# Two 16-head attention stages of a one-core transformer chain: the order of TensorE's products within a turn

## The chip, the cores and the metric

The kernel runs on one core of one Trainium2 chip. The metric is the device time in microseconds (us) of one execution. The other cores of the chip are not used. TensorE (PE in the profile, PEld for its weight loads), VectorE (DVE), ScalarE (ACT), GpSimd (POOL) and the DMA queue of SyncE (SP) each work through their own instructions in order and wait for one another by semaphores.

## The reference

The reference is a chain of eight blocks over x of 16 sequences x 256 positions x 128 features: four attention-like blocks and four feed-forward blocks, each with a layer norm ahead of it and behind it and a residual sum. Two of the eight have a 16-head causal attention with 8 features a head. The first of them (block five) is, cut to what matters:

```python
q = (x @ Wq).reshape(b, t, 16, 8) * 8 ** -0.25
k = (x @ Wk).reshape(b, t, 16, 8) * 8 ** -0.25
v = (x @ Wv).reshape(b, t, 16, 8)
dot = jnp.einsum('bqhd,bkhd->bhqk', q, k)
dot = jnp.where(causal, dot, -jnp.inf)
attn = jax.nn.softmax(dot, axis=-1)
out = jnp.einsum('bhqk,bkhd->bqhd', attn, v).reshape(b, t, 128) @ Wo
```

The second (inside block seven, behind a scan) has the same products with rotated and normalized queries and keys and with four key heads shared by the sixteen query heads. The change touches these two attentions alone.

## The kernel before

**Tiles.** The 16 sequences are handled as NG = 8 groups g of two sequences (512 positions). Within a group each sequence b = 0, 1 is one batch of attention. The 16 heads lie as 4 rows r of 32 partitions by 4 variants v of 8 features: `km` and `qm` (`variants`, line 377) are copies of the keys and queries, masked so that one variant's 8 features are left.

**One batch** (`attention`, line 434) has these steps; I give each group of TensorE products a name for the rest of the text.
- Scores by query (lines 449 to 461), three times (i = 0, 1, 2): four products, one a row, of 32 partitions, `qT` by `km`, each into a PSUM bank of its own (named Q in the prediction), then for each row a causal mask, added by a product of the identity with `negmask` (M), then VectorE's `tensor_reduce` for the maxima (`at_nm`).
- GpSimd splits the maxima into three bf16 pieces (`at_pc`, lines 464 to 469); TensorE transposes them and ScalarE makes four scaled copies (`at_mT`, lines 471 to 476).
- Scores by key (lines 481 to 502), three times: four products `kT` by `qm` (K), four that subtract the maxima, `ones` by `at_mT` (R), ScalarE's exponential into `at_e`, GpSimd's `affine_select` for the causal part.
- Values' products (lines 505 to 518; V): `at_vm` by `at_e`, each with 32 output partitions, into one PSUM bank "o", in six steps.
- ScalarE copies the bank to `at_oT` (line 521), TensorE transposes it (525), VectorE makes reciprocals and quotients (`at_rec`, `at_y`, lines 530 to 532), TensorE transposes `at_y` (537), ScalarE copies it to `at_yT`.

**PSUM.** Both stages use RING_BANKS (line 37): one bank "o" and a ring of seven banks "s" from which all other products take theirs in order. A product into a bank waits until the reader of the bank's last content is done.

**The order.** Each batch, each group's head and each tail is a Python generator; a `yield` ends a step. The head (`head`, line 1287 in the first stage and 1636 in the second) makes `kT`, `qT`, `km`, `qm` and `at_vm` of a group ahead of its batches; the tail (lines 1320 and 1662) multiplies with `Wo` and normalizes. `turns` (line 392) runs them: in each turn every item whose start has come runs its next step, in the order of the list, the latest batch first, then older batches, then heads, then one generator `beside`. Batch b of group g starts in turn 12g + 6b, so twelve turns are one group. Scores by query fall on even turns, scores by key on odd ones, values on both. The order in which the steps are run is the order of the instructions on every engine, since `manual_schedule` leaves it as it is. So an even turn of the steady part reads, on TensorE: Q, M, then values, then others; an odd turn: K, R, values, others. "Others" (X) are the transposes and projections of heads, tails and of the batches' last steps. Their places within the twelve turns are, in the first stage: `at_pc` and `at_y` in turns 2 and 8, `wk` 8, `wq` 9, `wo` 10, `at_oT` 5 and 11, `wv` and the transposes of `xn` 6. VectorE makes `at_y` in turns 1 and 7 and `xn` in turn 5.

The masks of one turn, before, follow their row's product:

```python
for k, s in zip(rows, ss, strict=True):
    self.mm(s, qT[k, q], km[k, vs, keys], True, False)
for r, s in enumerate(ss):
    ...
    self.mm(s[:, :, t * P :], ident, bc(negmask, 1, n), False, True)
    v_.tensor_reduce(nm[:, t, r, vs], s, AX.X, ALU.max, negate=True)
```

Of the kernel before, what the change touches and what calls it, by code (L numbers as in the profile page):

```python
# [29 lines left out]
NB, SEQ, P, D = 16, 256, 128, 128  # L30
NG, NT, GT = 8, 4, 512
# [154 lines left out]
def idle(n):  # L186

    for _ in range(n):
        yield


def bc(ap, axis, n):

    ap = ap.unsqueeze(axis)
    shape = list(ap.shape)
    shape[axis] = n
    return ap.to_broadcast(shape)


class Ctx:  # L200
# [188 lines left out]
        lo = 16 * (v % 2)  # L389
        self.nc.scalar.copy(to[:, :, :, lo : lo + 8], src)  # L390

    def turns(self, items):


        now = 0
        items = [[start, 0, steps] for start, steps in items]
        while items:
            for item in items[:]:
                for _ in range(min(3, now - item[0] + 1 - item[1])):
                    item[1] += 1  # L400
                    if next(item[2], self) is self:
                        items.remove(item)
                        break
            now += 1

    def attention_stage(self, head, early, first, tail, beside=iter(())):

        got = [{} for _ in range(NG)]
        heads = [head(g, got[g]) for g in range(NG)]
        for _ in range(first):
            next(heads[0])
        self.attention_pools()  # L420
        for _ in heads[0]:
            pass

        def batch(g, b):
            yield from self.attention(g, b, got[g])
            if b == 1:
                yield from tail(g, got[g]["yT"])

        items = [(12 * g + 6 * b, batch(g, b)) for g in range(NG) for b in range(2)]
        items = items[::-1] + [(12 * g - early, heads[g]) for g in range(1, NG)] + [(9, beside)]  # L430
        with self.tc.manual_schedule():
            self.turns(items)

    def attention(self, g, b, got):

        nc, v_ = self.nc, self.nc.vector
        vm = self.vm[g % 2]
        qT, kT, km = (got[n] for n in ("qT", "kT", "km"))
        ident, negmask, ones = self.cb["ident"], self.cb["negmask"], self.cb["rows"]
        q0, q1 = (slice((2 * b + t) * P, (2 * b + t + 1) * P) for t in range(2))
        both = slice(2 * b * P, (2 * b + 2) * P)
        rows = [slice(32 * r, 32 * r + 32) for r in range(4)]
        nm = self.t([P, 2, 4, 4], "at_nm", 2)
        for i in range(3):

            t, q, keys, vs = (0, q0, q0, slice(0, 4)) if i == 0 else (1, q1, both, slice(2 * i - 2, 2 * i))
            ss = [self.ps("s") for _ in rows]
            for k, s in zip(rows, ss, strict=True):
                self.mm(s, qT[k, q], km[k, vs, keys], True, False)
            for r, s in enumerate(ss):
                n = vs.stop - vs.start
                s = s.rearrange("p (v n) -> p v n", v=n)
                self.mm(s[:, :, t * P :], ident, bc(negmask, 1, n), False, True)
                v_.tensor_reduce(nm[:, t, r, vs], s, AX.X, ALU.max, negate=True)  # L459
            if i < 2:  # L460
                yield from idle(2)
        yield

        pc = self.pieces[b]
        for i in range(3):
            at = pc[:, :, :, 4 * i : 4 * i + 4]
            nc.gpsimd.tensor_copy(at, nm)
            if i < 2:
                nc.gpsimd.tensor_tensor(nm, nm, at, ALU.subtract)
        yield from idle(3)  # L470
        tp = self.ps("mm")
        for t in range(2):
            self.mm(tp[:, t * P : (t + 1) * P], pc[:, t].rearrange("p r n -> p (r n)"), ident, True, True)
        mT = self.t([P, 4, SEQ], "at_mT", 2, dt=BF16)
        for v in range(4):
            nc.scalar.activation(mT[:, v, :], tp[:, :SEQ], AF.Copy, scale=self.sel[:, v : v + 1])
        yield from idle(3)


        es, qm = [], got["qm"]  # L480
        for i in range(3):
            vs, to = (slice(2 * i, 2 * i + 2), slice(0, SEQ)) if i < 2 else (slice(0, 4), slice(P, SEQ))
            keys, queries = (q0, both) if i < 2 else (q1, q1)
            ss = [self.ps("s") for _ in range(4)]
            for k, s in zip(rows, ss, strict=True):
                self.mm(s, kT[k, keys], qm[k, vs, queries], True, False)
            for k, s in zip(rows, ss, strict=True):
                self.mm(s, ones[k, :], mT[k, vs, to], False, True)
            e = self.t([P, 4, GT], "at_e", 4)
            for r, s in enumerate(ss):  # L490
                nc.scalar.activation(e[:, r], s, AF.Exp)  # L491

            if i < 2:
                at, n = e.rearrange("p r (v t n) -> p r v t n", v=2, t=2)[:, :, :, 0, :], 2
            else:
                at, n = e.rearrange("p r (v n) -> p r v n", v=4), 4
            nc.gpsimd.affine_select(  # L497
                at, at, [[0, 4], [0, n], [1, P]], ALU.is_ge, 0.0, base=0, channel_multiplier=-1
            )
            es.append(e)  # L500
            if i < 2:
                yield from idle(2)
        yield

        o = self.ps("o")
        for v in range(4):
            reg = SEQ * (v // 2)
            for r, k in enumerate(rows):
                e = es[v // 2][:, r].rearrange("p (v n) -> p v n", v=2)[:, v % 2, :]
                self.mm(o[k, reg : reg + SEQ], vm[:, 2 * b, v, k], e, v == 0, False)  # L510
            yield
        for v in range(4):
            reg = SEQ * (v // 2)
            for r, k in enumerate(rows):
                e = es[2][:, r].rearrange("p (v n) -> p v n", v=4)[:, v, :]
                self.mm(o[k, reg + P : reg + SEQ], vm[:, 2 * b + 1, v, k], e, False, v % 2 == 1)
            if v % 2:
                yield

        oT = self.t([P, GT], "at_oT", 1)  # L520
        nc.scalar.copy(oT, o)  # L521
        yield
        tp = self.ps("mm")
        for j in range(4):
            nc.tensor.transpose(tp[:, j * P : (j + 1) * P], oT[:, j * P : (j + 1) * P], self.c["ident"])
        yield from idle(2)
        y = self.t([P, 2, 4, 2, 2, 8], "at_y", 2)
        tp = tp.rearrange("p (w t r u n) -> p w t r u n", w=2, t=2, r=4, u=2)
        rec = self.t([P, 2, 2, 4, 2], "at_rec", 2)
        v_.reciprocal(rec, tp[:, :, :, :, :, 8])  # L530
        for w in range(2):
            v_.tensor_tensor(y[:, :, :, w], tp[:, w, :, :, :, 0:8], bc(rec[:, w], 4, 8), ALU.mult)
        yield
        tp = self.ps("mm")
        for t in range(2):
            at = y[:, t].rearrange("p r w u n -> p (r w u n)")
            nc.tensor.transpose(tp[:, t * P : (t + 1) * P], at, self.c["ident"])
        if b == 0:
            got["yT"] = self.t([P, GT], "at_yT", 2)
        nc.scalar.copy(got["yT"][:, both], tp[:, :SEQ])  # L540
        yield
# [1545 lines left out]
```

## Time and profile before

| what | us |
|---|---|
| median of 3 runs | 2942.89 (2938.27 to 2943.25) |
| the profiled execution | 2940.6 |
| its span, first to last instruction | 2938.8 |
| busy: PE, DVE, ACT, POOL | 2729.7, 1953.3, 1717.5, 1017.2 |
| first attention stage, from its first masks to its last values | 1525.8 to about 1835 |
| second attention stage | 2326.2 to about 2640 |

Names in the profile are the program's tiles: `ps_s` is a bank of the ring, `ps_o` the values' bank. Nearly all products are issued by the helper at line 336, so they are told apart by their tiles. A shape such as 32*128 is rows by columns of the array that the product uses. A product of two float32 operands shows as two matmul instructions, so a group of four appears as x8. The end of a matmul is modelled; the distance from the start of one row to the start of the next is measured.

### The profile page before, as it was taken

The page shows a single profiled execution, that of the slowest core. Times are in us where ns is not written, and L with a number is a line of the kernel's source. Part 1 is how long each engine was busy: PE and PEld are TensorE (multiplying, and loading weights), DVE is VectorE, ACT ScalarE, POOL GpSimd, SP SyncE. Part 2 cuts the span into 40 slices and gives each one's busy share as a digit, 9 for nine tenths or more (in the row PEclk, how much of TensorE's full clock was granted, in tenths as well). Part 3 has the DMA queues.
Part 4 walks back from the last instruction along what each step waited for, and adds up shares of the span by engine and source line. Part 5 has one row for each costly group of instructions (what it writes and reads, how often), then busy time and mean ns, then how long its engine had stood idle before and what let it go on. Part 6 is the DMA issues. An engine that isn't in the chain of part 4 may idle for free.

```text
span 2938.8 us, 59589 instructions
## 1 busy us (share of the span) xinstructions
PE 2729.7 (93%) x23673; PEld 1845.0 (63%) x23674; DVE 1953.3 (66%) x5309; ACT 1717.5 (58%) x3568; POOL 1017.2 (35%) x1406
## 2 busy tenths in 40 slices
PE   8889999999998799999978998899999799989998
PEld 4556667766666588888853443566666444436897
DVE  5665666666675989999866765666574677736542
ACT  6756566666665567777735665444444277756443
POOL 3543333333345100000044555422231466545332
PEclk9999999999999899999988999899999899999999
DMA  4000000000000000000020000000000000010000
GB/s 117 12 1 1 2 1 2 2 2 2 5 12 24 1 16 9 8 9 8 9 71 5 1 1 1 1 1 1 1 1 1 2 1 1 1 33 27 2 16 16
DMA packets 29150, 31.30 MB, mean 11 GB/s; under 512 B 7292, under 2 KB 20156, under 8 KB 28732
## 3 DMA queue, kind: packets, MB, share of 16 engines
q1 hardware_dynamic: 28872, 27.49, 3.1%
q8 instruction: 187, 3.06, 0.4%
q14 instruction: 91, 0.75, 0.1%
HBM read 23.29 MB, written 4.19 MB: 9 GB/s over the span
## 4 chain that ended last, share of the span: by engine, by line
PE 69%; ACT 12%; DVE 11%; POOL 5%; issue 2%; DMA 0%; POOLq 0%; SPq 0%; ACTq 0%; DVEq 0%
PE ps_s L336 44%; PE ps_o L336 10%; PE ps_mm L336 6%; PE ps_s L325 3%; ACT e L949 2%; ACT at_e L491 1%; POOL ln_rs L245 1%; ACT lg L1215 1%; DVE xn L264 1%; PE ps_xin L336 1%; ACT meT L1222 1%; POOL e L952 1%; PE ps_sum L336 1%; ACT L949 1%; ACT mdisp L1122 1%
## 5 line engine op out<-in xcount | busy, mean ns | idle before, releaser
L459 DVE TENSOR_REDUCE at_nm<-ps_s 128x2 f32<-128x512 f32 (+1 forms) x384 | 238.1, 682 | 119.6 <-PE ps_s L336 119.6
L491 ACT ACTIVATE at_e<-ps_s 128x512 f32<-128x512 f32 x384 | 198.2, 604 | 97.0 <-PE ps_s L336 94.8
L1504 DVE TENSOR_TENSOR scan<-ps_s,lm 128x384 f32<-128x384 f32 x256 | 124.7, 549 | 142.4 <-PE ps_s L336 142.1
L497 POOL TENSOR_SCALAR_AFFINE_SELECT at_e<-at_e 128x1024 f32<-128x1024 f32 (+1 forms) x96 | 135.1, 1407 | 209.0 <-ACT at_e L491 208.7
L245 POOL TENSOR_TENSOR ln_rs<-ln_rs,mhalf 128x4 f32<-128x4 f32 x192 | 196.1, 1021 | 15.8
L1031 POOL TENSOR_TENSOR ln_rs<-ln_mv,mendt 128x4 f32<-128x4 f32 x6 | 1.2, 200 | 521.0 <-DVE ln_mv L1029 521.0
L244 POOL TENSOR_SCALAR ln_rs<-ln_mv 128x4 f32<-128x4 f32 x184 | 39.6, 215 | 371.2 <-DVE ln_mv L257 352.8
L336 PE MATMUL ps_o<-my,meT 128*128 128x129 f32 x1024 | 142.5, 286 | 22.2 <-ACT mgot L1234 18.4
L336 PE MATMUL ps_s<-l1f_phi,mxT 128*128 128x256 f32 x512 | 141.6, 401 | 21.6 <-DVE mpart L1096 15.9
L899 DVE TENSOR_REDUCE l_max<-ps_s 128x3 f32<-128x384 f32 x256 | 124.8, 551 | 51.4 <-PE ps_s L336 49.1
L952 POOL TENSOR_SCALAR_AFFINE_SELECT e<-e 128x512 f32<-128x512 f32 x128 | 78.9, 637 | 217.2 <-ACT e L949 217.2
L336 PEld LDWEIGHTS ps_o<-my,meT 128*128 128x128 f32 x1024 | 126.3, 193 | 40.5 <-ACT mgot L1234 24.1
L336 PE MATMUL ps_s<-qm,kT 32*128 32x512 f32 x768 | 144.0, 652 | 8.0 <-DVE at_nm L459 7.8
L336 PE MATMUL ps_s<-km,qT 32*128 32x512 f32 x768 | 138.2, 667 | 11.3 <-DVE qT L1648 3.7
L336 PEld LDWEIGHTS ps_o<-l_w,mlp_h 128*128 128x128 f32 x1024 | 126.0, 192 | 19.1 <-issue 12.8
L336 PE MATMUL ps_o<-at_e,at_vm 128*32 128x128 f32 (+1 forms) x2048 | 123.2, 338 | 15.3 <-ACT at_oT L521 15.3
L336 PE MATMUL ps_o<-l_w,mlp_h 128*128 128x128 f32 x1024 | 130.1, 276 | 4.0 <-ACT oT L969 3.9
L336 PE MATMUL ps_s<-b_negmask,b_ident 128*128 128x256 bf16 (+1 forms) x640 | 123.6, 303 | 8.1 <-DVE b_negmask L780 1.4
L1481 ACT COPY BT<-ps_s 128x512 f32<-128x512 f32 x64 | 37.5, 587 | 158.1 <-PE ps_s L336 158.1
L336 PE MATMUL ps_mm<-mdisp,mxn 128*128 128x128 f32 x1024 | 125.3, 279 | 5.0 <-DVE mdisp L1134 4.9
L336 PEld LDWEIGHTS ps_mm<-mdisp,mxn 128*128 128x128 f32 x1024 | 121.8, 195 | 7.9 <-DVE mdisp L1134 6.6
L336 PE MATMUL ps_s<-xT,l_w 128*128 128x512 f32 x256 | 124.4, 607 | 1.3 <-ACT xT L811 1.3
(469 smaller groups left out, 7192.5 us busy)
## 6 DMA issues: line engine op xcount, KB each, us to landing
mw<-in_l1fw SPq DMA_DIRECT2D x16, 256.0 KB, 2.6
moe_w<-in_moe SPq DMA_DIRECT2D x16, 256.0 KB, 5.3
l_w<-in_l SPq DMA_DIRECT2D x10, 256.0 KB, 3.3
x<-in_x SPq DMA_DIRECT2D x8, 256.0 KB, 5.1
xs<-x SPq DMA_DIRECT2D x8, 256.0 KB, 2.1
out<-x SPq DMA_DIRECT2D x8, 256.0 KB, 2.3
slT<-xs SPq DMA_DIRECT2D x6, 256.0 KB, 2.8
l1f_phi<-in_l1f SPq DMA_DIRECT2D x1, 1024.0 KB, 5.0
```

What stands on the lines that cost most here:

```text
L244: g.tensor_scalar(out, in_, scale, eps, ALU.mult, ALU.add)
L245: g.tensor_tensor(out, out, self.mhalf[:, :n], ALU.pow)
L325: self.nc.tensor.transpose(out[:n, k * P : (k + 1) * P], src[:, k, cols], self.c["ident"])
L336: self.nc.tensor.matmul(out, lhsT=lhsT, rhs=rhs, start=start, stop=stop, skip_group_check=True)
L459: v_.tensor_reduce(nm[:, t, r, vs], s, AX.X, ALU.max, negate=True)
L491: nc.scalar.activation(e[:, r], s, AF.Exp)
L497: nc.gpsimd.affine_select(at, at, [[0, 4], [0, n], [1, P]], ALU.is_ge, 0.0, base=0, channel_multiplier=-1)
L899: v.tensor_reduce(mx[:, b, :, h, 16], s, AX.X, ALU.max, negate=True)
L949: nc.scalar.activation(e[:, h].rearrange("p j n -> p (j n)"), s[:, : 3 * P], AF.Exp)
L952: nc.gpsimd.affine_select(e[:, :, j, :], e[:, :, j, :], [[0, 4], [1, P]], ALU.is_ge, 0.0, base=0, channel_multiplier=-1)
L1481: nc.scalar.copy(s, ps)
L1504: v.tensor_tensor(m, s[:, : SEQ + P], lm[:, SCAN_HEADS[4 * (t // 2) + 2 * i + hh], :], ALU.mult)
```

## The change

`turns` can be given, for even and for odd turns, an order of kinds. Each step now yields the kind of the step that follows it ("by query", "values", "by key", or None for others), and in each turn the items are sorted by that order (items of one kind keep the list's order). In even turns it is others, by query, values, by key; in odd ones values, by key, others, by query. So on TensorE an even turn becomes X, M, Q, V, and an odd one V, K, R, X: over two turns X, M, Q, V, V, K, R, X. Every step stays in its turn. Within a step of scores by query the four masks are now issued first (they start the bank) and the four products after them; the four reductions follow the four products. On VectorE the order of instructions in the steady part of the first stage stays as it was; on GpSimd the `affine_select` of an odd turn now stands ahead of the pieces `at_pc` of that turn. In the two instruction orders that are built, the array's tile shape changes 283 and 291 times between neighbouring products of the two stages before, and 195 times in each after.

```diff
@@ -389,21 +389,28 @@
         lo = 16 * (v % 2)
         self.nc.scalar.copy(to[:, :, :, lo : lo + 8], src)
-    def turns(self, items):
+    def turns(self, items, kinds=None):
         now = 0
-        items = [[start, 0, steps] for start, steps in items]
+        items = [[item[0], 0, item[1], item[2] if len(item) > 2 else None] for item in items]
         while items:
-            for item in items[:]:
+            order = items[:]
+            if kinds:
+                order.sort(key=lambda item: kinds[now % 2].index(item[3]))
+            for item in order:
                 for _ in range(min(3, now - item[0] + 1 - item[1])):
                     item[1] += 1
-                    if next(item[2], self) is self:
+                    item[3] = next(item[2], self)
+                    if item[3] is self:
                         items.remove(item)
                         break
             now += 1
     def attention_stage(self, head, early, first, tail, beside=iter(())):
@@ -426,10 +433,10 @@
             if b == 1:
                 yield from tail(g, got[g]["yT"])
-        items = [(12 * g + 6 * b, batch(g, b)) for g in range(NG) for b in range(2)]
+        items = [(12 * g + 6 * b, batch(g, b), "by query") for g in range(NG) for b in range(2)]
         items = items[::-1] + [(12 * g - early, heads[g]) for g in range(1, NG)] + [(9, beside)]
         with self.tc.manual_schedule():
-            self.turns(items)
+            self.turns(items, ([None, "by query", "values", "by key"], ["values", "by key", None, "by query"]))
     def attention(self, g, b, got):
@@ -450,16 +457,18 @@
             t, q, keys, vs = (0, q0, q0, slice(0, 4)) if i == 0 else (1, q1, both, slice(2 * i - 2, 2 * i))
             ss = [self.ps("s") for _ in rows]
+            n = vs.stop - vs.start
+            by_variant = [s.rearrange("p (v n) -> p v n", v=n) for s in ss]
+            for s in by_variant:
+                self.mm(s[:, :, t * P :], ident, bc(negmask, 1, n), True, False)
             for k, s in zip(rows, ss, strict=True):
-                self.mm(s, qT[k, q], km[k, vs, keys], True, False)
-            for r, s in enumerate(ss):
-                n = vs.stop - vs.start
-                s = s.rearrange("p (v n) -> p v n", v=n)
-                self.mm(s[:, :, t * P :], ident, bc(negmask, 1, n), False, True)
+                self.mm(s, qT[k, q], km[k, vs, keys], False, True)
+            for r, s in enumerate(by_variant):
                 v_.tensor_reduce(nm[:, t, r, vs], s, AX.X, ALU.max, negate=True)
+            yield
             if i < 2:
-                yield from idle(2)
-        yield
+                yield "by query"
         pc = self.pieces[b]
         for i in range(3):
@@ -474,7 +483,8 @@
         mT = self.t([P, 4, SEQ], "at_mT", 2, dt=BF16)
         for v in range(4):
             nc.scalar.activation(mT[:, v, :], tp[:, :SEQ], AF.Copy, scale=self.sel[:, v : v + 1])
-        yield from idle(3)
+        yield from idle(2)
+        yield "by key"
         es, qm = [], got["qm"]
@@ -499,8 +509,9 @@
             )
             es.append(e)
             if i < 2:
-                yield from idle(2)
-        yield
+                yield
+                yield "by key"
+        yield "values"
         o = self.ps("o")
         for v in range(4):
@@ -508,14 +519,14 @@
             for r, k in enumerate(rows):
                 e = es[v // 2][:, r].rearrange("p (v n) -> p v n", v=2)[:, v % 2, :]
                 self.mm(o[k, reg : reg + SEQ], vm[:, 2 * b, v, k], e, v == 0, False)
-            yield
+            yield "values"
         for v in range(4):
             reg = SEQ * (v // 2)
             for r, k in enumerate(rows):
                 e = es[2][:, r].rearrange("p (v n) -> p v n", v=4)[:, v, :]
                 self.mm(o[k, reg + P : reg + SEQ], vm[:, 2 * b + 1, v, k], e, False, v % 2 == 1)
             if v % 2:
-                yield
+                yield "values" if v == 1 else None
         oT = self.t([P, GT], "at_oT", 1)
         nc.scalar.copy(oT, o)
```

## Prediction

> **What bounds the kernel now.** I read the page first, then the stretches of the two stages that the change touches, then the order of work on PE, DVE and POOL inside one period.
>
> ```profile
> span 2938.8 us, 59589 instructions
> L459 DVE TENSOR_REDUCE at_nm<-ps_s 128x2 f32<-128x512 f32 (+1 forms) x384 | 238.1, 682 | 119.6 <-PE ps_s L336 119.6
> L491 ACT ACTIVATE at_e<-ps_s 128x512 f32<-128x512 f32 x384 | 198.2, 604 | 97.0 <-PE ps_s L336 94.8
> ```
>
> The profiled execution took 2940.6 us (span 2938.8); the median of the three runs is 2942.9, so this profile stands 0.1% below it. Both groups mostly wait for PE. The stages' steady parts confirm it (columns: length, busy PE, PEld, DVE, ACT, POOL, clock):
>
> ```profile
> 1593.38:1797.04 203.66, 201.16 (x1816) 89.63 (x1813) 141.31 (x321) 130.49 (x285) 110.63 (x152) 1.00 0.01 1
> 2394.48:2590.00 195.52, 190.35 (x1711) 86.29 (x1707) 136.58 (x216) 140.01 (x318) 116.72 (x138) 0.99 0.01 1
> ```
>
> PE is busy 97 to 99%, but a busy PE is not a full one. Its timeline (start, length; I call masks M, scores by query Q, scores by key K, their at_mT products R, values' products V, all else X):
>
> ```profile
> 1655.37 0.40 PE L336 MATMUL ps_s<-at_mT,b_rows 32*128 32x512 bf16 x4
> 1655.70 0.65 PE L336 MATMUL ps_o<-at_e,at_vm 128*32 128x128 f32 x16
> 1656.27 1.12 PE L336 MATMUL ps_s<-xT,l_wq 128*128 128x512 f32 x2
> 1657.33 1.14 PE L336 MATMUL ps_s<-km,qT 32*128 32x512 f32 x8
> 1658.40 0.61 PE L336 MATMUL ps_s<-b_negmask,b_ident 128*128 128x256 bf16 x4
> 1658.94 0.64 PE L336 MATMUL ps_o<-at_e,at_vm 128*32 128x256 f32 x8
> 1659.51 1.16 PE L336 MATMUL ps_s<-l_wo,at_yT 128*128 128x128 f32 x8
> 1660.60 1.55 PE L336 MATMUL ps_s<-qm,kT 32*128 32x512 f32 x7
> 1661.56 0.63 PE L336 MATMUL ps_s<-at_mT,b_rows 32*128 32x512 bf16 x3
> 1661.99 0.59 PE L336 MATMUL ps_s<-qm,kT 32*128 32x512 f32 x1
> ```
>
> The tile shape (32*128, 128*128, 128*32) changes at almost every row. From start to start: M 0.54 before V but 0.45 before another 128*128 group (1651.95 to 1652.40), so 0.09 goes to the change of shape; wo to K is 1.09 where eight products of that shape (l_wv, before more 128*128 work) take 0.995. I price a change at 0.095. The last three rows show the second loss: the fourth K is late, because its PSUM bank still awaits a DVE reduction. Such a split costs about 0.77 (K and R together 2.1 instead of 1.29); it occurs 18 times in 37 between 1580 and 1800 and 8 in 37 between 2380 and 2600.
>
> **The change part by part.** No instruction is added or removed. *Changes of shape*: the built order of PE has 283 of them in the first stage and 291 in the second, and 195 in each afterwards: 184 x 0.095 = -17.5 us if PE alone counted. Here two rules of the Trainium skill disagree. "TensorE: Matmul & The Clock Gate" (Part 2, NX overlap) has the drain of one matmul hide under the next one's fill: then the sum is 0. "TensorEngine Tiling" (Key Properties) says a change of mode drains the array. The rows above side with the second, so I take -17.5. *Masks ahead of the products*: same eight instructions; a late bank now delays a mask, which are serial anyway. But the four products now end together and the first reduction starts later. "TensorEngine Tiling" (PSUM Bottleneck) warns that tiling speeds PE and not the emptying of PSUM; by that rule the saved drains would buy nothing. The split K rows agree that banks already decide, so PE's saving must be checked against them, period by period.
>
> *The new order.* From the start of the masks in an even turn: M to Q 0.54 (0.97 with 512-wide masks), Q 1.07, two V groups 1.05 (0.57 + 0.48), K 0.96, R 0.33. All X of the odd and next even turn now follow at 3.95 (4.38). Others' cadence: reductions start 1.70 after the masks (Q's second pass at +0.53, its result 0.59 later, 0.04 to start) and take 0.60 each, so DVE reaches the odd turn's other work at 4.10 (4.53). Exponentials start 0.50 after R, one each 0.49, 0.60 long; their four banks free at 4.76, 5.25, 5.74, 6.23 (+0.43). The bank ring has seven "s" banks: with x banks of X between K and M, the fourth mask waits for K's bank number x.
>
> This puts X directly behind the DVE work of the odd turn, where before Q, M and V lay between:
>
> ```profile
> 1667.93 0.34 DVE L530 RECIPROCAL at_rec<-ps_s 128x32 f32<-128x32 f32 x1
> 1668.31 0.49 DVE L532 TENSOR_TENSOR at_y<-ps_s,at_rec 128x128 f32<-128x128 f32 x2
> 1714.22 1.89 POOL L383 TENSOR_TENSOR qm<-qT,const_head 128x1024 f32<-128x1024 f32 x1
> 1714.28 2.68 DVE L264 TENSOR_SCALAR xn<-x,ln_mv,ln_rs 128x128 f32<-128x128 f32 x4 [1.06 <-POOL ln_rs L245]
> ```
>
> at_y takes 0.87, so it is ready at 5.0 (5.45) while its transposes want to start near 4.1 (4.5): PE waits about 1 us, twice in twelve turns, and wk, M and Q queue behind it. xn takes 2.7 because its first operation stands as long as POOL's qm runs beside it; its chain is affine_select, ln_rs, xn.
>
> First stage, twelve turns, mask to mask. Before, from the trace (1665.10 to 1700.29): 4.81, 5.31, 5.18, 6.75, 6.45, 6.70 = 35.2. Afterwards:
> - turn 0: at_y bound, 5.45 + transposes 0.27, + 0.21 carried from turn 10 = 5.93 (before: none here);
> - turn 2: no X; 0.12 carried, fourth mask 0.43 late; 4.07;
> - turn 4: V waits for at_oT (fourth exponential, 0.62 copy) till 2.8; POOL gets to affine_select at 2.3, is done with it and ln_rs at 5.7, qm at 7.6, xn at 8.4 to 8.5, its transposes 0.44: 8.95;
> - turn 6: at_y again, then wk 0.86: 6.58;
> - turn 8: wq 0.86, wo 0.995, nothing late: 5.80;
> - turn 10: oT 0.44: 4.39, fourth mask 0.21 late.
> Sum 35.7. The same working applied to before gives 35.0, so the comparison is +0.5 to +0.7 a period. What is gained (no drain at X, the late K of turns 2, 8 and 10) is given back at the seams of turns 0, 4 and 6. 5.8 periods: +3.5 us.
>
> Second stage, before (2470.06 to 2506.11): 36.05. Afterwards: turn 0 5.93; the table load for the exponential (1.28, seen at 2473.05 once R is done) makes the banks and DVE 1.3 later, so turn 2, which waits for n behind qk's product (1.2 + 0.7), is 7.8; turns 4 to 10 are 5.46, 7.6 (rot, 0.94 + 0.68, ahead of kT's transposes), 5.39 and 4.39. Sum 36.5: +0.4 a period, 5.5 periods: +2.2 us.
>
> *Filling the stages* (1525.8 to 1593.4, 2326.2 to 2394.5), where PE is idle 10.4 of 67.6 us and 7.5 of 68.3: there reductions and other DVE work used to run while PE went ahead. Now a head's transposes stand ahead of M and Q on PE, so DVE work, X, M and Q (0.45 + 0.45 + 0.1 + 1.1 + 0.2, about 2.2 us) go in series where a normalized tile is due. No row shows it. Bounds: -2 us (heads start earlier), +15 us (seven such turns in series). I take +4, two turns' worth. The end of each stage has no Q; 0, bounds -2 and +2.
>
> Sum: 2940.6 + 3.5 + 2.2 + 4 = 2950.3; carried to the median (+2.3 us) 2952.6. I say 2952.
>
> **The rivals.**
> *A, the forecast*: the seams from odd to even turn give back more than the drains: 2952. Chance 0.40.
> *B, faster*: the seams are covered. Place: turn 4 of the first stage (xn) and turns 2 and 6 of the second (n, rot). Price: if xn misses qm on POOL it is ready 1.7 earlier (5.8 x 1.7 = 10 us), and if n and rot start among the reductions' gaps and not behind them, 2.6 a period (14 us): 2952 - 24 = 2928. It decides where DVE's result lands before PE has ended R and at_pc. For it: DVE is only 70% busy. Against: DVE and POOL keep their order, and xn lost to qm in every steady period of this trace. If late banks vanish as well, 2915. Chance 0.25.
> *C, no difference*: drains and seams cancel, or the change of shape costs PE nothing that banks would not cost as well: 2943. Chance 0.18.
> *D, slower yet*: filling runs in series as its upper bound, and each seam carries over into the next one: 2952 + 11 + 6 = 2969. Chance 0.17.
>
> **How the numbers follow.** 0.2%, about what a measurement can tell from no change, is 6 us. Faster is B, 0.25; same is C and a little of A, 0.20; slower is the rest, 0.55. The range goes from B's middle to D: 2920 to 2972; A alone spans 2944 to 2960.
>
> **What would show it.** In the changed profile: two V groups in a row with 1.05 to the next K; K no longer split in seven and one; idle or long starts of PE at const_ident,at_y with DVE at_y as the releaser, about 1 us and some 30 times; const_ident,xn waiting for DVE xn in the first stage; a twelve-turn period of 35.5 to 36.3 in the first stage. Wrong if that period falls under 35 (then B), if the second V group costs its own drain (no saving), or if the gaps lie in the filling (then D).

## The result and the profile after

The changed kernel takes 2974.57 us (median of four executions, 2973.95 to 2977.14) against 2940.7 us before (four executions, three of them those of the table above): 1.0112 times as long, interval 1.010 to 1.0125, or 34 us more. The direction was forecast, and the size was not: the sum said +9 to +11, and 2974.57 lies outside the range of 2920 to 2972.

On the page of the profiled execution the two groups that mostly wait for PE wait longer (the last columns: idle time ahead of the group, and what ended it). The reductions wait 182.0 us in place of 119.6, the exponentials 192.3 in place of 97.0:

```profile
span 2975.0 us, 59550 instructions
...
L468 DVE TENSOR_REDUCE at_nm<-ps_s 128x2 f32<-128x512 f32 (+1 forms) x384 | 238.1, 682 | 182.0 <-PE ps_s L336 181.9
L501 ACT ACTIVATE at_e<-ps_s 128x512 f32<-128x512 f32 x384 | 198.2, 603 | 192.3 <-PE ps_s L336 190.2
```

The windows of the two stages, from the masks of turn 24 to the last masks (columns as in the prediction). The first row answers to the prediction's first, which was 203.66 long with PE busy 201.16. PE is now idle for 22 us of 215, and its clock is below 1.00:

```profile
1599.20:1814.28 215.08, 193.06 (x1823) 87.09 (x1821) 137.65 (x321) 129.47 (x287) 112.12 (x158) 0.97 0.01 1
2421.05:2636.40 215.35, 190.59 (x1823) 89.24 (x1821) 136.64 (x229) 146.30 (x336) 117.52 (x144) 0.97 0.01 1
```

I cut each trace at the first scores by query, at those of turn 24, at the last ones, and at the last at_y. Call the parts filling, steady part and end. In us:

| | ahead of stage 1 | stage 1: filling, steady, end | stage 2: filling, steady, end |
|---|---|---|---|
| before | 1524.7 | 67.6, 203.6, 35.7 = 306.9 | 69.2, 206.9, 32.2 = 308.2 |
| changed | 1531.3 | 69.0, 214.5, 34.9 = 318.5 | 80.2, 214.8, 33.6 = 328.6 |
| changed, second trace | 1528.3 | 68.8, 211.8, 34.9 = 315.5 | 80.2, 214.8, 33.6 = 328.6 |

Each row is one execution; the same instructions can give a stage a few us more or less (first stage here, second stage in run 9). So the first stage gives 9 to 12 us of the 34 and the second 20, and 2 to 5 stay without a place. The 4 to 7 us ahead of both stages belong mostly to single executions: with the same instructions up to there, but for the four masks that now stand first (1 us), the kernels of this study reach this point anywhere between 1522.7 and 1531.3.

Where the first stage loses its time is seen in turn 4, where xn's transposes stand ahead of the masks. The timeline (start, length; idle time ahead and its releaser in brackets):

```profile
1725.88 1.07 PE L336 MATMUL ps_o<-at_e,at_vm 128*32 128x256 f32 x16 [0.61 <-ACT at_oT L532]
1726.88 1.14 PE L336 MATMUL ps_s<-qm,kT 32*128 32x512 f32 x8
...
1728.79 1.89 POOL L383 TENSOR_TENSOR qm<-qT,const_head 128x1024 f32<-128x1024 f32 x1
1728.85 3.48 DVE L264 TENSOR_SCALAR xn<-x,ln_mv,ln_rs 128x128 f32<-128x128 f32 x4 [1.08 <-POOL ln_rs L245]
...
1730.91 0.30 PE L325 MATMUL ps_s<-const_ident,xn 128*128 128x128 f32 x1 [1.19 <-DVE xn L264]
...
1731.87 0.84 PE L325 MATMUL ps_s<-const_ident,xn 128*128 128x128 f32 x3 [0.66 <-DVE xn L264]
...
1732.55 1.03 PE L336 MATMUL ps_s<-b_negmask,b_ident 128*128 128x512 bf16 x4
```

The reader is to see two things. Sixteen values' products take 1.00 to the next scores by key (1.05 was forecast): the grouping works. And POOL's qm and DVE's xn start together, xn takes 3.48 us, and PE stands 1.85 us in front of its transposes, with the masks of the next turn behind them.

### The profile page after: what moved, and what is told of

Its sections match the earlier page's. It is cut to its first block, busy times and chain, and to the rows that moved or that the text cites. A ratio compares the mean times of both kernels' runs of the same rounds, so it can differ in the third digit from the quotient of the medians.

```text
span 2975.0 us, 59550 instructions
## 1 busy us (share of the span) xinstructions
PE 2711.3 (91%) x23674; PEld 1844.7 (62%) x23674; DVE 1938.0 (65%) x5309; ACT 1711.8 (58%) x3568; POOL 1013.3 (34%) x1406
## 4 chain that ended last, share of the span: by engine, by line
PE 65%; DVE 14%; ACT 13%; POOL 5%; issue 2%; DMA 0%; POOLq 0%; ACTq 0%; SPq 0%; DVEq 0%
PE ps_s L336 41%; PE ps_o L336 9%; PE ps_mm L336 6%; PE ps_s L325 3%; DVE at_nm L468 2%; ACT at_e L501 2%; ACT e L960 2%; POOL ln_rs L245 2%; DVE xn L264 2%; ACT lg L1226 1%; ACT meT L1233 1%; PE ps_xin L336 1%; POOL e L963 1%; PE ps_sum L336 1%; ACT L960 1%
## 5 line engine op out<-in xcount | busy, mean ns | idle before, releaser
L468 DVE TENSOR_REDUCE at_nm<-ps_s 128x2 f32<-128x512 f32 (+1 forms) x384 | 238.1, 682 | 182.0 <-PE ps_s L336 181.9
L501 ACT ACTIVATE at_e<-ps_s 128x512 f32<-128x512 f32 x384 | 198.2, 603 | 192.3 <-PE ps_s L336 190.2
L336 PE MATMUL ps_s<-l1f_phi,mxT 128*128 128x256 f32 x512 | 142.9, 404 | 22.0 <-DVE mpart L1107 16.5
L336 PE MATMUL ps_s<-b_negmask,b_ident 128*128 128x256 bf16 (+1 forms) x640 | 137.8, 311 | 21.9 <-ACT at_e L501 10.6
L336 PE MATMUL ps_s<-qm,kT 32*128 32x512 f32 x768 | 134.9, 666 | 10.8 <-DVE at_nm L468 10.8
L336 PE MATMUL ps_s<-km,qT 32*128 32x512 f32 x768 | 120.2, 698 | 2.0 <-POOL km L383 1.3
L264 DVE TENSOR_SCALAR xn<-z,ln_mv,ln_rs 128x128 f32<-128x128 f32 x252 | 74.9, 359 | 70.1 <-POOL ln_rs L245 70.1
```

What stands on the lines that cost most here:

```text
L264: self.nc.vector.tensor_scalar(out[:, k, :], src[:, k, :], mv[:, k, 0:1], rs[:, k : k + 1], ALU.subtract, ALU.mult)
L336: self.nc.tensor.matmul(out, lhsT=lhsT, rhs=rhs, start=start, stop=stop, skip_group_check=True)
```

## The experiments

S was the theory that other products, now right behind the DVE work that they need, hold masks and scores behind them (the seams). Its rivals were the masks' new place (R1), the grouping itself (R2), and drains that never counted (R3). All times are medians, with the ratio to the kernel before run beside them; the lengths of stages are from one trace each.

**1. The two halves of the change, and the seam undone.** The first kernel keeps the order of the turns before:

```diff
-            self.turns(items, ([None, "by query", "values", "by key"], ["values", "by key", None, "by query"]))
+            self.turns(items)
```

> The changed kernel with the order of the turns as before, so that only the masks stand ahead of the scores by query. PE's built order has 280 and 283 changes of tile shape in the two stages (before 283 and 291), so drains explain at most 1 us. Theory S (seams: other products in even turns stand right behind the DVE work that they need, and masks and scores queue behind them): the masks cost little, 2938 to 2948. Rival R1 (masks first: the four products end together, reductions start about 0.5 us later and banks are held longer): at least half of the 34 us, 2957 or more.

2952.45 us, ratio 1.0038 (1.0026 to 1.0051). Between the two expectations: stage 1 306.4, stage 2 314.8. The steady parts are 5.0 and 5.8 us longer, and the first filling and end 3.3 and 2.1 shorter. The masks first are not free in the old order, but they are not the 34 us.

The second kernel has the new order, and in each group of four the masks behind the scores as before.

> The changed kernel with the masks behind the scores by query as before, so that only the order of the kinds is new. PE's order has 224 and 234 changes of shape (changed kernel 195 each), 68 x 0.095 = 6 us of drains more. Theory S: the seams are all there, 2968 to 2985. Rival R1 (masks first costs most): under 2957. Rival R3 (drains cost PE nothing that banks would not): equal to the changed kernel within 3 us, 2972 to 2978, where S with drains at their price gives 2980.

2991.81, ratio 1.0167 (1.0153 to 1.0181); stages 323.2 and 342.1. The order alone costs more than the whole change. R1 falls, and so does R3's equality. But 17 us between this kernel and the changed one are also far more than the 6 of its drains; the eighth run shows why.

The third moves one entry:

```diff
-[None, "by query", "values", "by key"]
+["by query", None, "values", "by key"]
```

> The changed kernel with one entry moved: in even turns scores by query stand first and the other products second. Masks first, values back to back and the odd turns stay. 223 and 226 changes of shape. Theory S: at_y, xn, n and rot have 1.5 us more (masks and scores run in between), all seams but half of xn and rot are covered, and what is left is the saved drains, (283-223 + 291-226) x 0.095 = 12 us: 2928 to 2948. Rival R2 (the grouping itself, exponentials' banks that come free late for the next masks) or R1: the time stays at 2965 or more.

2938.9, ratio 0.9991 (0.9984 to 0.9998); stages 302.0 and 311.4. This is S's number: 36 us go with one entry, while masks first and the grouped values stay.

The fourth has the new order only in the first stage.

> The changed kernel with the new order of kinds in the first of the two stages only; masks first in both. The traces put +12 us on the first stage, +18 on the second and +4 to +6 ahead of both. Theory S: 2941 + 12 plus at most 4 for the masks in the second stage, 2950 to 2958. If the seams only cost through the filling of the second stage: under 2948. If the masks are the cost (R1): 2965 or more.

2959.76, ratio 1.0063 (1.005 to 1.0076), 2 us over S's range; stages 318.0 and 314.5. The second stage is that of the masks alone, within 0.3. The stages add up, and the second one's loss is the greater.

**2. Which seam, which part, and the clock.** In the fifth kernel only the heads' steps (and those beside) go behind the scores by query in even turns. They get a kind of their own:

```diff
+    [None, "by query", "head", "values", "by key"], ["values", "by key", None, "head", "by query"]
```

> The changed kernel in which, in even turns, only the heads' other products (transposes of xn, n and rot with their DVE work, wk, wq, qkv) stand behind the scores by query; the batches' own (at_oT, at_y, wo) stay ahead of masks and scores. Moving both took 36 us off. Theory S splits this by the waits in the trace: at_y 0.52 us twice a period, 11 periods, 11 us; xn 1.85 us a period in six periods, 11 us; the filling of the second stage up to 12 us; n and rot the rest. So 25 us come back: 2945 to 2955. Rival: the batches' at_y seam is the greater one (it is met twice as often): 2960 or more.

2944.45, ratio 1.0007 (0.9999 to 1.0015); stages 304.8 and 311.9. A little more came back than the 25 expected: 30 of the 36 us hang on the heads' steps (xn, n, rot and the products behind them). The batches' steps, with at_y, where PE still waits its 0.52 us, keep 6 by the medians and 3 by the stages of the traces.

The sixth keeps the old order of turns up to turn 13:

```diff
-            if kinds:
+            if kinds and now >= 14:
```

> The changed kernel with the order of the turns before kept for turns 0 to 13 of each stage; masks first throughout. The filling took 13.5 us longer in the second stage and 1.3 us in the first. Theory F (other products ahead of masks make the fill run in series): 10 us or more come back, 2958 to 2966. Rival (the fill only shifts, the heads are late by as much anyway and the loss returns in the following turns): 2970 to 2976.

2961.78, ratio 1.0062 (1.0048 to 1.0075). 13 us come back. By the traces 6.5 of them are in stage 2 (its filling is 72.7 in place of 80.2); stage 1 is 3.3 under the first trace of the changed kernel and 0.3 under the second. F holds for stage 2.

The seventh adds filler products:

```diff
+        for _ in range(n):    # 2 ahead of at_y's transposes, 6 ahead of xn's, n's and rot's
+            self.mm(out, self.cb["ident"], bc(self.cb["negmask"], 1, 4))
```

> The changed kernel with filler products (bf16, 128x512, into the bank that the transposes behind them overwrite) ahead of the transposes that wait: 2 before at_y, 6 before xn, n and rot from the second group on. They run while PE would wait, and leave out nothing. Theory C (the clock at half speed after PE's new waits is a cost of its own): the half-clock windows of the steady parts go, the intervals of 8.1 to 8.5 us become 6.6, and the filling of the second stage runs at a higher clock: 2955 to 2968. Rival (half clock falls where PE waits anyway): 2971 to 2980.

2964.69, ratio 1.0074 (1.006 to 1.0089), inside C's range, but only half of C is shown. Stage 1 is 311.9, 3.6 to 6.6 under the two traces without fillers, and its intervals of 8.1 to 8.5 are gone. Stage 2 is 329.0, as it was. Its filling is 79.4 long at a clock of 0.87 as it was 80.2 at 0.77: there the chain of n's operations is what PE waits for. In its steady part the fillers have a price of their own: the scores of turn 8 follow those of turn 6 after 7.87 in place of 6.77 in four periods. So this run can't say what the clock costs there. The rest of the 10 us is in neither stage (by the trace the first scores come at 1525.3, 6 us earlier) and can't be credited to the fillers. What the clock costs is seen in two windows of the changed kernel that hold the same 48 products (turn 6 to turn 8; the clock is the column before the last two):

```profile
1618.61:1626.75 8.14, 7.62 (x48) 2.68 (x47) 3.23 (x7) 2.26 (x5) 0.46 (x2) 0.79 0.01 3
1732.55:1739.19 6.64, 6.12 (x48) 2.40 (x47) 3.23 (x7) 2.54 (x6) 0.46 (x2) 1.00 0.00 0
```

The 1.5 us between them are the clock alone: DVE's busy time is the same 3.23, and PE is idle for the same 0.52.

The eighth has the seam undone and the masks behind the scores.

> The seam undone (in even turns scores by query, then other products) and the masks again behind the scores. 192 and 202 changes of shape, 55 fewer than with masks first, 180 fewer than before: 5 and 17 us if drains count. Masks first cost 9.7 us in the old order of turns. Theory S with drains at their price: 2918 to 2930, faster than both kernels. Rival R3 (drains cost nothing that the banks would not): 2929 or more, with masks last worth up to 10 us all the same; if masks first helps in any grouped order, as it did by 17 us with the seams: 2945 or more.

2955.82, ratio 1.0041 (1.0028 to 1.0055). I was wrong: with 55 fewer changes of shape it is 17 us slower than the same order with masks first (stages 305.2 and 320.7 against 302.0 and 311.4). The rows of PE show it. A bank that comes free late now breaks up the four scores, which run side by side when they start together:

```profile
1706.71 0.60 PE L336 MATMUL ps_s<-km,qT 32*128 32x512 f32 x3
1707.13 0.60 PE L336 MATMUL ps_s<-km,qT 32*128 32x512 f32 x3
1707.90 1.12 PE L336 MATMUL ps_s<-km,qT 32*128 32x512 f32 x2 [0.16 <-ACT at_e L501]
1708.95 0.61 PE L336 MATMUL ps_s<-b_negmask,b_ident 128*128 128x256 bf16 x4
```

From the first scores to the masks go 2.24 us in place of 1.07. By the starts in the traces, at full clock, the last of a group's eight instructions starts over 0.7 us after the first (0.55 when nothing is late) in 44 of 45 groups of the first stage and 42 of 43 of the second. With masks first (run 3) it does so in none of 47 and 44: there the late bank delays one mask.

**3. The collision on POOL.** The ninth kernel is the changed one with one move in the head of the first stage:

```diff
-        yield from idle(6)
+        yield from idle(8)
         got["qm"] = k.variants(got["qT"], "qm")
-        yield from idle(2)
```

> The changed kernel in which POOL's qm of the first stage is issued two turns later, behind the turn of xn; xn's transposes stay ahead of masks and scores. Theory P (qm beside xn is what makes xn late: its first operation stands 1.9 to 2.2 us in place of 0.35): PE's waits of 1.19 and 0.66 us in front of xn's transposes go down by about 1.6 together, in six periods, and some half-clock windows with them: 10 us off the first stage (318.5 from its first scores to its last at_y), 2962 to 2967. Rival: xn is late through affine_select and ln_rs on POOL all the same: first stage 315 or more, 2970 to 2976.

2958.07, ratio 1.0046 (1.0032 to 1.0061). Stage 1 is 301.4, 14 to 17 us less, more than the 10 of theory P. (Stage 2, where no instruction differs from the changed kernel, is 331.7 in this trace, 3.1 more, with a filling of 84.2.) Turn 4 again:

```profile
1713.94 1.12 DVE L264 TENSOR_SCALAR xn<-x,ln_mv,ln_rs 128x128 f32<-128x128 f32 x4 [1.08 <-POOL ln_rs L245]
1714.63 0.80 PE L325 MATMUL ps_s<-const_ident,xn 128*128 128x128 f32 x4
1715.28 1.03 PE L336 MATMUL ps_s<-b_negmask,b_ident 128*128 128x512 bf16 x4
```

xn takes 1.12 in place of 3.48, PE doesn't wait, and the interval from turn 4 to turn 6 is 7.06 in place of 9.41; the period of twelve turns falls from 36.2 to 33.8.

Theory P named one collision, but there are two. Of xn's four pieces qm holds up the first, in the kernel before as well. In the changed kernel the second one is held up too, by an `affine_select`. The first two rows are of the changed kernel, with the second piece alone; the last one is of the four pieces before (shortest, median and longest, in ns):

```profile
1730.64 1.09 POOL L507 TENSOR_SCALAR_AFFINE_SELECT at_e<-at_e 128x1024 f32<-128x1024 f32 x1
L264 DVE TENSOR_SCALAR xn<-x,ln_mv,ln_rs x1: 1126/1126/1126, 1730.7 to 1730.7; 128x128 f32<-128x128 f32 x1
L264 DVE TENSOR_SCALAR xn<-x,ln_mv,ln_rs x4: 335/336/1915, 1714.3 to 1716.6; 128x128 f32<-128x128 f32 x4
```

The change itself did this: it put the `affine_select` ahead of at_pc, and so right behind qm. Every trace with the new order of kinds and qm in its old place has 3.47 or 3.48 for xn in each steady period; before and with the masks alone it is 2.68 or 2.69. The later qm takes away both, 1.57 and 0.79 us by these durations, which are the 2.35 between 9.41 and 7.06. The `affine_select` was not moved by itself.

The tenth run is the changed kernel again.

> The changed kernel once more, for a second trace. If its first scores by query, 1531.3 in the first trace and 1524.7 in the kernel before, come at 1531 again, something ahead of both stages belongs to the change; if they come elsewhere between 1523 and 1531, as in the other kernels, those 6 us are a difference between executions. The two stages should last 318 and 328 us within 2.

One execution, 2971.23. Its stages are in the table above: the second repeats to 0.1, the first is 3.0 shorter, with two steady intervals at a lower clock (7.84 and 7.64) in place of three, and the first scores come at 1528.3.

Is the collision a cost of the change, or of both kernels? The eleventh run makes the same move in the kernel before.

> The kernel before with qm of the first stage two turns later and nothing else. In the changed kernel this took the first stage from 318.5 to 301.4 us, under the 306.9 of before. Theory P (in the order before, xn's late end is hidden behind masks, scores and values, and only the changed order lays it bare): first stage 305 to 308, 2938 to 2944. Rival: the later qm helps any order, and the grouping itself gains nothing in the first stage: 300 to 303, 2936 to 2938.

2940.84, ratio 0.9989 (0.9983 to 0.9996). Stage 1 is 300.6, 6.3 less than before, and 2.7 of that lie in the filling. So P was wrong that before hides it all, though the total lies in its range. By the medians the move gains 16.5 us in the changed kernel and 3.6 in the one before. With qm out of the way the change costs 0.8 us in the first stage (301.4 against 300.6), and with it 9 to 12: eight to eleven of those are the two collisions and the clock that goes with them. The new order does gain in the steady part, 33.8 in an undisturbed period against 34.65, though only 198.4 us against 200.0 in all, and gives it back in the filling (68.0 against 64.9).

**4. The second stage.** The twelfth kernel brings n's operation two turns forward from the third group on:

```diff
-        ... [(12 * g - early, heads[g]) for g in range(1, NG)] ...
+        ... [(12 * g - early - 2 * (early == 26 and g > 1), heads[g]) for g in range(1, NG)] ...
     v.tensor_tensor(n, xa, bc(rs, 2, D), ALU.mult)
-    yield
+    yield from idle(1 + ahead)    # ahead is 2 for g > 1
```

> The changed kernel in which, from the third group of the second stage on, the heads start two turns earlier and n's transposes wait two turns longer behind n's DVE operation; all that follows stays at its turn. Theory S: PE's wait of 2.08 us at n's transposes goes in five periods, the interval of 8.0 us becomes 6 or less, second stage 328.6 - 10 = 319, 2960 to 2966. Rival: the interval is set by the exponentials' banks that the table load delays (the masks wait 0.56, 0.22 and 0.22 us for them), and n's place on DVE only delays something else: second stage 325 or more, 2969 or more.

2965.47, ratio 1.0066 (1.0054 to 1.0078). Stage 2 is 316.4, 12.2 less: 6.2 in the filling, 6.0 in the steady part. The changed kernel's rows first, two from its filling and one from the steady part; then the new one's rows at that place of the steady part:

```profile
2351.23 1.11 PE L325 MATMUL ps_s<-const_ident,n 128*128 128x128 f32 x4 [7.26 <-DVE n L1596]
...
2355.10 1.06 PE L336 MATMUL ps_s<-b_negmask,b_ident 128*128 128x256 bf16 x4
...
2361.54 0.63 PE L325 MATMUL ps_s<-const_ident,n 128*128 128x128 f32 x4 [3.10 <-DVE n L1596]
...
2514.17 0.63 PE L325 MATMUL ps_s<-const_ident,n 128*128 128x128 f32 x4 [2.08 <-DVE n L1596]
```

```profile
2502.82 0.66 PE L325 MATMUL ps_s<-const_ident,n 128*128 128x128 f32 x4
2503.31 0.57 PE L336 MATMUL ps_s<-b_negmask,b_ident 128*128 128x256 bf16 x3
2504.10 0.27 PE L336 MATMUL ps_s<-b_negmask,b_ident 128*128 128x256 bf16 x1 [0.22 <-ACT at_e L501]
```

The second masks of the stage come at 2355.10, behind the second group's n, 15.8 us after the first ones; before, they came after 3.8 us. That wait stays in the new kernel, whose second group is untouched (run 6, which has the old order there, takes it away: the second masks come after 4.6 us). The waits of 3.10 and 2.08 for later groups' n are gone. Turn 2 to turn 4 falls from 8.00 to 5.87 in one period and to 7.44 in two others. PE is idle for 1.00 us in all three; the two longer ones hold a stretch of half speed (the third column from the end):

```profile
2420.31:2427.75 7.44, 6.44 (x62) 3.00 (x60) 4.27 (x7) 4.30 (x11) 1.11 (x1) 0.77 0.01 2
2497.44:2503.31 5.87, 4.87 (x63) 2.32 (x61) 3.86 (x7) 4.30 (x11) 1.94 (x2) 1.00 0.01 3
2532.30:2539.74 7.44, 6.44 (x62) 3.09 (x60) 4.78 (x7) 4.29 (x11) 1.96 (x2) 0.77 0.00 0
```

8 of the second stage's 20 us remain; the banks behind the table load were not tried by themselves.

**5. Putting the parts together.** First the seam undone in the first stage, with the second stage as before.

> First stage: masks first, scores by query, other products, then values, scores by key, other products (it lasted 302.0 us in that form). Second stage as in the kernel before, masks behind the scores (308.2). If stages add up: 5 us under before, 2934 to 2940, first stage 301 to 303, second 307 to 309. If the second stage depends on how the first leaves clock and queues: second stage 311 or more and no gain.

2940.94, ratio 0.9995 (0.9987 to 1.0003). Its stages are 302.0 and 308.4 as expected, but over its executions no gain can be told: the traced one took 2935.59, 5 us less than the median.

Then the seam undone in the second stage too, from turn 14 on, and the four squares of the first group two turns later.

> As the last one, but the second stage takes the new order with masks first from turn 14 on, and the four squares of the first group's output (ACT, once per run) come two turns later, away from the two loads of ACT's tables, so that the exponentials behind them are not 2.1 us later and the one interval of 11.9 us (8.6 before) shrinks to 8 or less. Second stage 308.2 - 5.5 x 0.4 = 306 or, with the squares' interval better than before as well, 304: 2930 to 2937. Rival: ACT has no free place for them, and an interval elsewhere grows as much: second stage 309 or more, 2938 or more.

2937.31, ratio 0.9981 (0.9971 to 0.9991), just over what I expected: stage 2 is 307.4, 0.9 under before, where I expected 304 to 306. The squares' interval does fall to 6.45 (11.92 in run 3, 8.64 before) and the steady part to 203.4 from 206.9, but the end is 2.5 us longer than before.

Last, this with the changed kernel's order in the first stage from turn 14 on, and the later qm.

> First stage: masks first and the changed kernel's order from turn 14 on, scores by query ahead of other products before that, qm two turns later. Second stage as in the version with the later squares (307.4). Filling of the first stage 5 us shorter than with the later qm alone: first stage 296 to 298 (before 306.9), in all 11 us under before, 2929 to 2934. Rival: what the filling gains is waited for later: first stage 301 to 302, 2935 to 2938.

2933.45, ratio 0.9961 (0.9949 to 0.9974): 11 us under the kernel before beside it, the fastest version of the study. By its trace it is so otherwise than I said. Stage 1 is 301.6, not 296 to 298 (the rival's number: filling 66.8, one steady interval at a lower clock), and stage 2 is 304.7, 2.7 less than expected. That the total came as expected is luck.

## Why the prediction was right in sign and wrong in size

**Order and steady period: right.** The twelve turns worked out by hand against an undisturbed period of the changed kernel (from 1713.12 and 2500.78):

| turn | 0 | 2 | 4 | 6 | 8 | 10 | sum |
|---|---|---|---|---|---|---|---|
| stage 1 forecast | 5.93 | 4.07 | 8.95 | 6.58 | 5.80 | 4.39 | 35.7 |
| stage 1 measured | 5.92 | 4.10 | 9.41 | 6.64 | 5.75 | 4.38 | 36.2 |
| stage 2 forecast | 5.93 | 7.8 | 5.46 | 7.6 | 5.39 | 4.39 | 36.5 |
| stage 2 measured | 5.86 | 8.00 | 5.76 | 7.19 | 5.28 | 4.44 | 36.5 |

(The forecast terms of stage 2 add up to 36.6, not 36.5.) The step "xn at 8.4 to 8.5, its transposes 0.44" made turn 4 0.5 late: it counts qm's hold on xn and not that of the `affine_select` behind it, 0.79. Rival B named its price ("if xn misses qm on POOL it is ready 1.7 earlier (5.8 x 1.7 = 10 us)"), and the move gave 14 to 17: it frees xn of the `affine_select` as well, and the steady part of its trace has no half speed.

**Drains: right that they count; no run gives their price by itself.** "184 x 0.095 = -17.5 us" is 1.2 us a period; with the collisions gone, an undisturbed period gains 0.8, and the masks' new place is in that. The better pair is run 1 and run 3, both with masks first: 57 changes of shape fewer in each stage, 5.4 us at that price, and steady parts 5.0 and 5.2 us shorter. Other waits can have moved between these two as well.

**Masks first: "which are serial anyway" was half of it.** Where scores would start together a late bank costs less on a mask: 17 us in either grouped order. But in the old order masks first make the steady parts 5.0 and 5.8 us longer. There the last K of a group starts over 0.7 us after the first in 34 of 47 and 30 of 46 groups (before 26 of 45 and 22 of 46, all at full clock), so more banks are late. The later start of the reductions, which I had named and priced at nothing, is a likely reason; no run shows it by itself.

**The step that failed is the sum from one undisturbed period to a stage.** Three terms:
- *"5.8 periods: +3.5 us" and "5.5 periods: +2.2 us."* Measured in the steady parts: +10.9 and +8.0. In the first stage the undisturbed period explains 1.0 x 5.8 = 5.8. Three intervals at a lower clock (8.13, 8.48 and 8.09 for 6.64) add 4.8; a second trace has two, elsewhere. That term, PE's own new waits turned into a slower clock, was not in my sum at all. The second steady part is 5.8 periods as well, not 5.5. The undisturbed period gives 0.5 x 5.8 = 2.8, two turns of 7.18 and 7.05 for 5.76, again at a lower clock, give 2.7, and the once-in-a-run turn with the squares gives 2.4 more than it cost before (13.09 over an ordinary 8.00, against 8.64 over 5.98).
- *Filling: "I take +4, two turns' worth."* Measured +1.4 and +11.0, 12.5 together, inside my bounds of -2 and +15 and near the upper one. Masks and scores do queue behind n, as the part said. The wait at the first n alone is 7.26 us, where I had priced about 2.2 us for a turn, because the whole chain of squares, root and product is still ahead of n at that time.
- *The end of the stages:* -0.7 and +1.4, within the bounds given.

The account for the profiled execution: forecast 2950.3; steady parts 18.9 for 5.7, +13.2; filling 12.5 for 4, +8.5; ends +0.6; ahead of the stages +6.5, of which the parts between and behind them give 2.3 back: together 2976.8, against 2977.1 measured. So A's mechanism was right, with the filling of rival D and a clock that no case had.

**What I said would show it.** The period of 36.2 lies in the range named, 35.5 to 36.3. The last K is still late, counted as above in 14 of 45 and 18 of 44 groups (before 26 of 45 and 22 of 46), so the late banks are fewer and have not gone. At_y, which I named first, is the smallest of the seams: PE waits 0.52 us for it and not about 1, and the fifth kernel puts it, with the batches' other steps, at 6 us in all (2944.45 - 2938.9).

## What to carry to other kernels

Grouping products of one tile shape does save PE time, but only as long as nothing that PE must wait for is put ahead of work that is ready. Before reordering, list for every transposed operand who makes it and how late, and keep the ready work (here masks and scores) between the two. Look, too, at what the new order puts side by side on other engines: here one `affine_select`, moved by a few places, held up a normalization. A forecast from one clean period has to be completed by the filling, by turns that happen once in a run, and by the clock that new waits bring.

## What the runs showed of the hardware

**The clock follows busy time in fixed windows.** In every trace of this study half speed comes in stretches of 3.41 us or multiples, and all their edges lie on one grid of 3.41 us through the whole trace. These are grid windows of the changed kernel; the first three are followed by half speed, the last is not:

```profile
1615.59:1619.00 3.41, 1.57 (x8) 0.78 (x8) 2.80 (x4) 1.73 (x7) 3.12 (x7) 0.99 0.00 0
1653.13:1656.55 3.42, 0.62 (x6) 0.41 (x4) 2.21 (x2) 1.96 (x9) 3.34 (x4) 0.99 0.00 0
1765.77:1769.19 3.42, 1.57 (x8) 0.77 (x7) 2.76 (x4) 1.72 (x7) 3.13 (x7) 0.99 0.00 0
1728.23:1731.64 3.41, 1.79 (x14) 1.43 (x13) 2.79 (x2) 2.73 (x8) 3.41 (x3) 1.00 0.00 0
```

Take the windows at full speed of both steady parts of this trace. The six that are followed by half speed have PE busy 1.57 us or less, and all others 1.79 or more: the edge lies near half. It isn't sharp by this measure: in the second trace a window with 1.82 is followed by half speed and one with 1.75 is not. The Trainium skill ("TensorE: Matmul & The Clock Gate", Part 1) gives the same free-running window of about 3.4 us, but has the clock fall after an idle window; further on it tells of a kernel whose clock swings because of frequent short pauses, without a figure. Here PE's longest wait in the first and third window was 1.2 us, so two short waits that fall in one window (1.17 and 0.67 in the first) are enough. Whether they do depends on how the program lies on the grid: the two traces of one kernel have three and two such windows in the steady part of the first stage, with 4.8 and 2.2 us of longer intervals, most of the 3 us between them.

**Long operations of POOL hold up xn, and not the reductions.** One piece of xn of 128x128 takes 0.34 us alone, 1.91 beside qm and 1.13 beside the `affine_select`; in the kernel with the later qm, four reductions take 2.48 us beside qm, as they do elsewhere. The Trainium skill ("SBUF — State Buffer", Who interferes with whom) has the rule: DVE and POOL share a pair of SBUF ports, which a `tensor_scalar` from SBUF to SBUF can take and an operation with at most one SBUF input otherwise doesn't, and the one that comes second stands for the whole instruction. The rows agree where xn comes second: it starts 0.06 us after qm and ends its first piece 0.08 after it, and the second piece ends 0.08 after the `affine_select`. POOL's short operations beside the third and fourth piece (0.21 and 0.25 us, at_pc and at_nm) leave these at 0.34.
